# Moving the output projection, the layer norm and the convolution within a step, one PSUM bank for all attention sums, and other forms of a scan and a copy

## The chip, the cores and the metric

The kernel runs on one core of a Trainium2 chip. The metric is the time on the device for one execution, in microseconds (us); less is better. TensorE (PE), VectorE (DVE), ScalarE (ACT), GpSimd (POOL) and SyncE (SP) each work through a queue of their own in order; SP only issues DMAs here.

## The reference, cut to what matters

x has 16 images of 128 channels and 64 x 64 positions, so 4096 tokens each. Layer 0 is a group norm and a Mamba block, added to x. Layer 1 is an attention whose sums run over all earlier tokens, and then a routed feed-forward network (64 experts choose 8 tokens each).

```python
# layer 0: Mamba, 256 inner channels, 16 states
xz = gn(x) @ W_in; xs, z = split(xz)
xc = silu(causal_conv(xs, 4 taps) + conv_b)
dt, B, C = split(xc @ W_xproj)
delta = softplus(dt @ W_dt + b_dt)
h[t] = exp(delta[t]*A)*h[t-1] + (delta[t]*xc[t])*B[t]     # 16 states, 256 channels
y[t] = sum_n h[t]*C[t];  out = ((y + xc*D) * silu(z)) @ W_out;  x = x + out
# layer 1: attention with running sums, 8 heads
kv = silu(ln(t) @ W_kv);  s = q . k
m = cummax(s); e = exp(s - m); u = cumsum(e); w = cumsum(e*v)
t = t + mean_over_heads(w / u)
# then the routed feed-forward, added to t
```

## The kernel before

Three phases follow one another: layer 0 with the attention of layer 1 beside it (up to about 10090 us), the routing, and the experts with the final sums. The change touches the first phase alone.

**Steps.** A block is 512 tokens of one image; there are 16 x 8 = 128. The loop over `k` makes one step for each block, with the 16 states as its inner rounds `n`. In step k stand the scan of block k (`cur`), the end of layer 0 for block k - 1 (`prev`), the convolution and projections of block k + 1 (`nxt`), the attention of block m = k - 9 (`m`, whose second half ends in the next step as `mp_`), and the layer norm of block k - 8 (`mn`). So steps 0 to 8 have no attention; some ten steps at the end have no scan.

**A round.** In round n VectorE makes `bx` = delta*xc*B (`product`), then two scans of 512 tokens (`h`, one for each half of the channels). Between the two scans stands what `between(n)` emits: `score_less` at n = 4, `score_sum` at n = 6, `delta_x` at n = 15. POOL multiplies h with C into the tile `da`, which held the decay before, and copies the last column of h to `state`. At odd n `add_pair` has a DMA of POOL's queue add da of n - 1 to da of n; `add_y` lets TensorE turn and sum it into PSUM two rounds later. `decays` has ScalarE make the exponentials of up to two coming rounds; the variable LEAD limits how far ahead (8 rounds, in 13 da buffers). The queue of SP loads B and C of round n + 3 (`load_bc`, tile `bct`), 512 KB each.

**Everything else** is emitted by `beside(n)`, after `product(n)` and before the scans of the round. Each engine executes it in the order in which it is written, which was fixed by hand (`InOrder`), so the order of the calls is the order of each queue. What the prediction follows:

- `key`, `score`: keys of eight heads, then 32 x 2 small matmuls into `s_ps`; `score_max` (a running maximum, `mx`) and `score_less` on VectorE, `score_exp` on ScalarE, `score_sum` (a running sum, `sum`) on VectorE. Both running values are chained over chunks by `from_chunks` (two transposes, small scans on `z_max` or `z_sum`, and a copy of two columns).
- `score_log`, `rest`, `split`: the logarithm of the sums, and its split in three bf16 parts, which go back and forth between ScalarE and TensorE; `inverse` makes `e`; `turn_weights` turns the weights (`et_ps`); `store_parts` writes the parts to DRAM on ACT's queue, `spread_parts` reads them back on SP's queue with 16 small DMAs into `lh` and `rh`.
- `weights(c)` for each of four chunks: matmuls of lh and rh into two PSUM banks, exponentials by ScalarE into `wm`. `attend(c)`: 8 matmuls with wm, 16 small ones and one with `carry` for the sum over earlier chunks (`carry_ps`); `carry_on(c)` is its copy on ScalarE. `attend_before`, `add_x` and `finish` end a half of 256 tokens.
- `conv(nxt, a)`, eight matmul instructions for each half of the channels (`xs_ps`), `conv_silu` (tile `xc`), `xproj` (`dbl_ps`), `delta` (`dt_ps`), `gate_silu` (tile `z`).
- `turn_y` (`yb_ps`), `gate` (on VectorE, tile `z`), `out_proj` (`o_ps`, with the residual added by an identity matmul) and `put_back`, its copy on ScalarE.
- `ln_center`, `ln_square`, `ln_var`, `ln_scale` (tile `rstd`), `ln_apply` (tile `xn`, on VectorE): the keys of the next step read xn.

**PSUM.** Of eight banks three rotate as `bank(...)` for short results, two hold y, two hold bx, and one (`acc`) holds either the scores or the attention sums, one tile after the other.

Of the kernel before, what the change touches and what calls it, by code (L numbers as in the profile page):

```python
# [8 lines left out]
F32 = mybir.dt.float32  # L9
# [6 lines left out]
P = 128  # L16
# [23 lines left out]
def conv_attn_hybrid(ctx: ExitStack, tc: tile.TileContext, x, w_in, conv_w, conv_b, w_xproj, w_dt, b_dt,  # L40
# [40 lines left out]
    with ExitStack() as st:  # L81
        wp = st.enter_context(tc.tile_pool(name="wp", bufs=1))
        ps = st.enter_context(tc.tile_pool(name="ps", bufs=3, space=PSUM))
        acc = st.enter_context(tc.tile_pool(name="acc", bufs=1, space=PSUM))
# [49 lines left out]
        negc = wp.tile([P, 1], F32, name="negc")  # L134
        zs = {what: [wp.tile([P, 32], F32, name=f"z_{what}{a}") for a in range(2)] for what in ("max", "sum")}
# [70 lines left out]
        dap = st.enter_context(tc.tile_pool(name="dap", bufs=13))  # L206
# [92 lines left out]
        def gate_silu(k):  # L299
            w = blocks[k]  # L300
            z = w["z"] = m1.tile([P, NH2, L], F32, tag="z", name="z")
            for a in range(NH2):
                pt = bank("z_ps")
                PE.matmul(pt, wz[:, bass.ts(a, P)], w["xb"][:, KC - 1 :], start=True, stop=True)
                ACT.activation(z[:, a, :], pt, AF.Silu)
# [16 lines left out]
        def delta(k):  # L322
            w = blocks[k]
            d = w["delta"] = mp.tile([P, NH2, L], F32, tag="delta", name="delta")
            for a in range(NH2):
                pt = bank("dt_ps")
                PE.matmul(pt, wdt[:, bass.ts(a, P)], w["dbl"][:R, :], start=True, stop=True)
                softplus(d[:, a, :], pt, bdt[:, a : a + 1])
# [159 lines left out]
        def score(m, g):  # L488

            s = att[m]  # L490
            if g == 0:
                s["s"] = acc.tile([P, L], F32, tag="acc", name="s_ps")
            kt = [s.pop(("kt", 4 * g + j)) for j in range(4)]
            for c in range(CB):
                for j in range(4):
                    PE.matmul(s["s"][32 * j : 32 * j + 32, :P], q1[:, j, g, c, :], kt[j][:, bass.ts(c, P)],
                              start=(g == 0 and c == 0), stop=(g == 1 and c == CB - 1))

        def from_chunks(m, what, local, first, op0, op1, data):

            b, i = divmod(m, NBLK)
            last = stp.tile([P, 32], F32, tag=f"last_{what}", name=f"last_{what}")
            DVE.transpose(last, local[:, P - 32 :])
            z = zs[what][m % 2]
            if i == 0:
                DVE.memset(z[:, 0:10:5], first)
            else:
                DVE.tensor_copy(z[:, 0:10:5], gn[b][what][:, 4:14:5])  # L510
            gn[b][what] = z
            for g in range(2):
                DVE.tensor_tensor_scan(z[:, 5 * g + 1 : 5 * g + 5], bc(data[:, 0:1], [P, CB]),
                                       last[:, 5 * g : 5 * g + 4], z[:, 5 * g : 5 * g + 1], op0, op1)
            back = stp.tile([P, 32], F32, tag=f"back_{what}", name=f"back_{what}")
            DVE.transpose(back, z)
            return back[:, 31:32]

        def score_max(m):
            s = att[m]  # L520
            s["mx"] = a1.tile([P, P], F32, tag="mx", name="mx")
            DVE.tensor_tensor_scan(s["mx"], bc(negc, [P, P]), s["s"][:, :P], NEG, ALU.max, ALU.max)

        def score_less(m):
            s = att[m]
            mx = s.pop("mx")
            before = from_chunks(m, "max", mx, NEG, ALU.max, ALU.max, negc)
            x = s["x2"] = a1.tile([P, 2, P], F32, tag="x2", name="x2")
            DVE.scalar_tensor_tensor(x[:, 0, :], mx, before, s["s"][:, :P], ALU.max, ALU.subtract)
# [6 lines left out]
        def score_sum(m):  # L536
            s = att[m]
            s["sum"] = a1.tile([P, P], F32, tag="sum", name="sum")
            DVE.tensor_tensor_scan(s["sum"], bc(ones[:, 0:1], [P, P]), s["w"], 0.0, ALU.mult, ALU.add)
            s["before"] = from_chunks(m, "sum", s["sum"], 0.0, ALU.mult, ALU.add, ones)  # L540
# [25 lines left out]
        def rest(m, part):  # L566

            s = att[m]
            if part == 1:
                s["rest"] = bank("rest_ps")  # L570
                PE.matmul(s["rest"][:, : 2 * P], ident, s["x2"].rearrange("p w s -> p (w s)"), start=True, stop=False)
            PE.matmul(s["rest"][:, : 2 * P], minusb, s["parts"][:, part - 1].rearrange("p w s -> p (w s)"), start=False,
                      stop=True, skip_group_check=part > 1)
# [48 lines left out]
        def attend(m, c):  # L622
# [3 lines left out]
            if c % 2 == 0:  # L626
                s["o"] = acc.tile([P, L], F32, tag="acc", name="ao_ps")
# [44 lines left out]
        LEAD, LEAD_BC = 8, 3  # L672
# [37 lines left out]
        for k in range(NK + LAG + 1):  # L710
# [23 lines left out]
            def beside(n):  # L734
# [39 lines left out]
                if n == 4:  # L774
                    load_exp()
                    if m is not None:
                        score_max(m)
                    if mp_ is not None:
                        weights(mp_, 2)
                    if ends is not None:  # L780
                        gn_end(ends, 1)
                if n == 5:
                    if mp_ is not None:
                        attend(mp_, 2)
                        weights(mp_, 3)
                    if m is not None:
                        score_exp(m)
                    if prev is not None:
                        out_proj(prev)
                    decays(k, n, 2)  # L790
                    if mp_ is not None:
                        carry_on(mp_, 2)
                if n == 6:
                    if mp_ is not None:
                        attend(mp_, 3)
                        attend_before(mp_, 2)
                    if nxt is not None:
                        conv(nxt, 0)
                    decays(k, n, 2)
                    if prev is not None:  # L800
                        put_back(prev)
                    if mp_ is not None:
                        carry_on(mp_, 3)
                    if ends is not None:
                        gn_end(ends, 3)
                if n == 7:
                    if mp_ is not None:
                        attend_before(mp_, 3)
                        add_x(mp_, 1)
# [4 lines left out]
                    if m is not None:  # L814
                        split(m, 1)
                    if nxt is not None:
                        conv(nxt, 1)
                    if m is not None:
                        rest(m, 2)
                        inverse(m)  # L820
                    if mp_ is not None:
                        finish(mp_, 1)
                    if m is not None:
                        split(m, 2)
                        store_parts(m)
                    if nxt is not None:
                        conv_silu(nxt)
                    if ends is not None:
                        gn_end(ends, 4)
                if n == 8:  # L830
                    if m is not None:
                        turn_weights(m)
                        value(m, 0, 0)
# [3 lines left out]
                    if m is not None:  # L837
                        value(m, 0, 1)
                if n == 9:
                    if mn is not None:  # L840
                        ln_center(mn)
                        ln_square(mn)
# [6 lines left out]
                if n == 10:  # L849
                    if mn is not None:  # L850
                        ln_var(mn)
                    if nxt is not None:
                        delta(nxt)
                    load_exp()
                    if mn is not None:
                        ln_scale(mn)
                if n == 12:
                    if m is not None:
                        weights(m, 0)
                if n == 13:  # L860
                    if m is not None:
                        attend(m, 0)
                        attend_before(m, 0)
                        weights(m, 1)
                    decays(k, n, 2)
                    if m is not None:
                        carry_on(m, 0)
                if n == 14:
                    if mn is not None:
                        ln_apply(mn)  # L870
# [3 lines left out]
                    if m is not None:  # L874
                        carry_on(m, 1)
                if n == 15:
                    if stat is not None:
                        gn_stats(*stat)

            for n in range(N):  # L880
# [5 lines left out]
                if n in (4, 11, 12, 15):  # L886
                    decays(k, n, 2)
# [13 lines left out]
                if 8 <= n <= 11 and i == 0 and prev is not None:  # L901
                    store_residual(b - 1, n - 8)
                if 14 <= n <= 15 and i == 0 and cur is not None:
                    load_residual(b, n - 14)
                if n < 2 and i == 1 and cur is not None:
                    load_residual(b, n + 2)
                if n == 7 and mn is not None:
# [302 lines left out]
```

## Time and profile before

| what | us |
|---|---|
| median of 3 runs | 10935.1 |
| lowest and highest | 10931.48 and 10961.1 |
| profiled execution | 10931.22 |
| its span | 10929.5 |

The span runs from the first to the last instruction. The profile gives for each group of instructions its count, its mean duration and what ended the idle time ahead of it; the timeline gives single instructions as start, duration, engine, line, operation, output and inputs. Every operation of the first phase bears the line of the helper `InOrder` (L31), so rows are told apart by tiles. Adjacent instructions of one kind are merged to a row with their count; a 32-bit matmul counts as two. A TensorE row's end is modelled, and rows overlap a little; distances from start to start are safer.

### The profile page before, as it was taken

The page shows a single profiled execution, that of the slowest core. Times are in us where ns is not written, and L with a number is a line of the kernel's source. Part 1 is how long each engine was busy: PE and PEld are TensorE (multiplying, and loading weights), DVE is VectorE, ACT ScalarE, POOL GpSimd, SP SyncE. Part 2 cuts the span into 40 slices and gives each one's busy share as a digit, 9 for nine tenths or more (in the row PEclk, how much of TensorE's full clock was granted, in tenths as well). Part 3 has the DMA queues.
Part 4 walks back from the last instruction along what each step waited for, and adds up shares of the span by engine and source line. Part 5 has one row for each costly group of instructions (what it writes and reads, how often), then busy time and mean ns, then how long its engine had stood idle before and what let it go on. Part 6 is the DMA issues. An engine that isn't in the chain of part 4 may idle for free.

```text
span 10929.5 us, 157776 instructions
## 1 busy us (share of the span) xinstructions
PE 9405.6 (86%) x55389; PEld 5549.3 (51%) x55389; DVE 9012.1 (82%) x9987; ACT 7284.5 (67%) x12924; POOL 7530.3 (69%) x4771
## 2 busy tenths in 40 slices
PE   4579998899988989998899999989899899888875
PEld 2345555555555555555555555555555555544752
DVE  8998888888888888888889888888888888820753
ACT  5567776777777777777777777777777777754640
POOL 7887777778777777777777777777777777820000
PEclk7789998999999999899998998999999899999886
DMA  7777767777677777776777777677777777721348
GB/s 191 199 205 182 198 178 199 181 193 184 179 199 181 195 179 195 185 195 181 187 190 184 194 181 200 176 199 180 193 187 176 198 178 192 184 65 34 109 154 343
DMA packets 944361, 1995.67 MB, mean 183 GB/s; under 512 B 103040, under 2 KB 188688, under 8 KB 936400
## 3 DMA queue, kind: packets, MB, share of 16 engines
q1 hardware_dynamic: 732912, 1414.88, 43.6%
q0 software_dynamic: 129024, 469.82, 22.0%
q10 hardware_dynamic: 81632, 100.88, 2.7%
q8 instruction: 439, 7.19, 0.3%
q14 instruction: 354, 2.90, 0.1%
HBM read 1363.98 MB, written 151.52 MB: 139 GB/s over the span
## 4 chain that ended last, share of the span: by engine, by line
PE 61%; ACT 18%; DVE 7%; DMA 7%; issue 5%; SPq 1%; ACTq 1%; POOL 1%; DVEq 0%; POOLq 0%
PE ao_ps L31 10%; PE k_ps L31 8%; PE v_ps L31 7%; PE xs_ps L31 7%; PE y_ps L31 6%; ACT da L31 5%; PE carry_ps L31 4%; PE o_ps L31 4%; DVE h L31 3%; PE s_ps L31 3%; ACT L219 3%; ACT wm L31 2%; PE dt_ps L31 2%; DVE bx L31 2%; PE dbl_ps L31 2%
## 5 line engine op out<-in xcount | busy, mean ns | idle before, releaser
L31 POOL TENSOR_TENSOR da<-h,bct 128x1024 f32<-128x1024 f32 x2048 | 6475.5, 3162 | 1943.1 <-DVE h L31 1521.5
L31 DVE TENSOR_TENSOR_SCAN h<-da,state,bx 128x512 f32<-128x512 f32 x3584 | 4414.6, 1265 | 169.5 <-DVE bx L31 3.4
L31 DVE TENSOR_TENSOR bx<-du,bct 128x1024 f32<-128x1024 f32 x2048 | 2598.3, 1269 | 470.3 <-DMA bct<-bcs 404.1
L31 ACT ACTIVATE da<-delta,a_neg 128x512 f32<-128x512 f32 x4096 | 2629.8, 716 | 89.5 <-DMA da<-da 61.4
L31 PE MATMUL y_ps<-ident,da 128*128 128x128 f32 x9216 | 1428.1, 309 | 279.2 <-DMA da<-da 278.9
L31 PEld LDWEIGHTS y_ps<-ident,da 128*128 128x128 f32 x9216 | 1210.5, 160 | 719.6 <-issue 401.8
L31 PE MATMUL ao_ps<-wm,v 128*128 128x128 f32 x8192 | 1266.4, 318 | 281.5 <-ACT wm L31 276.4
L31 PEld LDWEIGHTS ao_ps<-wm,v 128*128 128x128 f32 x8192 | 1182.1, 226 | 559.8 <-ACT wm L31 401.8
L31 PE MATMUL v_ps<-wv,xn 128*128 128x512 f32 x2048 | 1035.8, 629 | 257.0 <-ACT xc L31 240.9
L31 ACT ACTIVATE v<-v_ps 128x512 f32<-128x512 f32 x1024 | 606.3, 597 | 778.7 <-PE v_ps L31 669.1
L31 ACT ACTIVATE wm<-w_ps 128x512 f32<-128x512 f32 x1024 | 552.1, 590 | 608.7 <-PE w_ps L31 607.3
L31 PE MATMUL k_ps<-xn,wk 128*128 128x512 f32 x2048 | 944.4, 595 | 1.7 <-ACT kt L31 1.7
L31 PE MATMUL xs_ps<-xb,wc 128*128 128x512 f32 x2048 | 925.3, 595 | 1.8 <-issue 1.8
L31 POOL DMA_DIRECT2D da<-da x896 | 787.7, 879 | 163.9 <-POOL state L31 95.1
L31 PEld LDWEIGHTS v_ps<-wv,xn 128*128 128x128 f32 x2048 | 341.9, 192 | 787.5 <-issue 316.1
L31 ACT ACTIVATE kt<-k_ps 128x512 f32<-128x512 f32 x1024 | 587.3, 600 | 190.0 <-PE k_ps L31 166.2
L31 DVE TENSOR_TENSOR_SCAN h<-da,bx 128x512 f32<-128x512 f32 x512 | 599.8, 1206 | 25.5 <-ACT da L31 0.5
L31 PEld LDWEIGHTS xs_ps<-xb,wc 128*128 128x128 f32 x2048 | 372.0, 191 | 397.1 <-issue 382.5
L31 ACT ACT_TABLE_LOAD x395 | 506.8, 1283 | 51.6 <-ACT parts L31 45.9
L31 PEld LDWEIGHTS k_ps<-xn,wk 128*128 128x128 f32 x2048 | 371.6, 191 | 321.0 <-issue 254.7
L31 POOL COPY state<-h 128x2 f32<-128x2 f32 x1792 | 509.0, 284 | 0.0
L31 DVE TENSOR_TENSOR z<-yb_ps,z 128x512 f32<-128x512 f32 x256 | 164.8, 685 | 339.7 <-PE yb_ps L31 339.3
(196 smaller groups left out, 10931.1 us busy)
## 6 DMA issues: line engine op xcount, KB each, us to landing
bct<-bcs SPq DMA_DIRECT2D x2048, 512.0 KB
da<-da POOLq DMA_DIRECT2D x896, 512.0 KB, 8.1
xs<-t_d SPq DMA_DIRECT2D x240, 256.0 KB
xs<-in_x_dram SPq DMA_DIRECT2D x128, 256.0 KB
xt<-in_x_dram SPq DMA_DIRECT2D x64, 512.0 KB
t_d<-xt SPq DMA_DIRECT2D x64, 512.0 KB
t_d<-xs ACTq DMA_DIRECT2D x256, 128.0 KB
t<-t_d SPq DMA_DIRECT2D x128, 256.0 KB
```

What stands on the lines that cost most here:

```text
L31: return lambda *args, **kw: self.tc.keep_in_program_order(f(*args, **kw))
L219: tc.keep_in_program_order(nc.scalar.preload_act_table_set(EXP_LN))
```

## The change

All calls of the diff stay what they compute; what differs is where they stand, which buffers they use, and the form of two VectorE operations.

- One PSUM tile `shared` takes the place of `acc` and lives through the phase: its first 256 columns hold the attention sums and `rest`, the third 128 the scores, the last 128 zeros, written once.
- The running sum adds w and those zeros; it no longer reads a broadcast column of ones from SBUF. The copy in `from_chunks` becomes a reduction over an axis of length one.
- In `beside`: the convolution's halves go from n = 6 and 7 to n = 4 and 6, `out_proj` and `put_back` from n = 5 and 6 to n = 10, the layer norm from n = 9, 10 and 14 to n = 13, 14 and 15, `weights(m, 0)` from n = 12 to 11, `attend(m, 0)` and `attend(m, 1)` from n = 13 and 14 to n = 12 and 13. The last half of the attention of the block before ends at n = 6 and not at n = 7. At n = 7 `conv_silu` stands ahead of `turn_weights` and the second split.
- `delta` issues its matmuls for both halves, then both softplus.
- z has two buffers, da has 12, LEAD is 7.
- Loads and stores of the residual and one load of x stand in other rounds.

```diff
-        acc = st.enter_context(tc.tile_pool(name="acc", bufs=1, space=PSUM))
+        bank1 = st.enter_context(tc.tile_pool(name="bank1", bufs=1, space=PSUM))
...
+        shared = bank1.tile([P, L], F32, name="shared")
+        nc.vector.memset(shared, 0.0)
...
-        dap = st.enter_context(tc.tile_pool(name="dap", bufs=13))
+        dap = st.enter_context(tc.tile_pool(name="dap", bufs=12))
...
-            z = w["z"] = m1.tile([P, NH2, L], F32, tag="z", name="z")
+            z = w["z"] = m1.tile([P, NH2, L], F32, tag="z", name="z", bufs=2)
...
+            pt = [bank("dt_ps") for _ in range(NH2)]
             for a in range(NH2):
-                pt = bank("dt_ps")
-                PE.matmul(pt, wdt[:, bass.ts(a, P)], w["dbl"][:R, :], start=True, stop=True)
-                softplus(d[:, a, :], pt, bdt[:, a : a + 1])
+                PE.matmul(pt[a], wdt[:, bass.ts(a, P)], w["dbl"][:R, :], start=True, stop=True)
+            for a in range(NH2):
+                softplus(w["delta"][:, a, :], pt[a], bdt[:, a : a + 1])
...
-                s["s"] = acc.tile([P, L], F32, tag="acc", name="s_ps")
+                s["s"] = shared[:, 2 * P : 3 * P]
...
-                DVE.tensor_copy(z[:, 0:10:5], gn[b][what][:, 4:14:5])
+                DVE.tensor_reduce(z[:, 0:10:5], gn[b][what][:, 4:14:5].unsqueeze(2), mybir.AxisListType.X, ALU.max)
...
-            DVE.tensor_tensor_scan(s["sum"], bc(ones[:, 0:1], [P, P]), s["w"], 0.0, ALU.mult, ALU.add)
+            DVE.tensor_tensor_scan(s["sum"], s["w"], shared[:, 3 * P :], 0.0, ALU.add, ALU.add)
...
-                s["rest"] = bank("rest_ps")
+                s["rest"] = shared
...
-                s["o"] = acc.tile([P, L], F32, tag="acc", name="ao_ps")
+                s["o"] = shared
...
-        LEAD, LEAD_BC = 8, 3
+        LEAD, LEAD_BC = 7, 3
```

The order in `beside` after the change, from n = 4, the conditions left out:

```python
n == 4:  load_exp(); score_max(m); weights(mp_, 2); conv(nxt, 0); decays; gn_end(ends, 1)
n == 5:  attend(mp_, 2); score_exp(m); carry_on(mp_, 2); attend_before(mp_, 2); weights(mp_, 3); decays
n == 6:  conv(nxt, 1); attend(mp_, 3); attend_before(mp_, 3); add_x(mp_, 1); decays
         carry_on(mp_, 3); finish(mp_, 1); gn_end(ends, 3)
n == 7:  score_log(m); rest(m, 1); decays; split(m, 1); inverse(m); conv_silu(nxt)
         turn_weights(m); rest(m, 2); split(m, 2); store_parts(m); gn_end(ends, 4)
n == 8:  xproj(nxt); store_bc(nxt); value(m, 0, 0), value(m, 0, 1)
n == 9:  gate_silu(cur); load_block(k + 2, ACT); value(m, 1, 0), value(m, 1, 1)
n == 10: delta(nxt); out_proj(prev); load_exp(); put_back(prev)
n == 11: weights(m, 0); decays
n == 12: attend(m, 0); attend_before(m, 0); carry_on(m, 0); weights(m, 1); decays
n == 13: ln_center(mn); ln_square(mn); attend(m, 1); decays; carry_on(m, 1)
n == 14: ln_var(mn); ln_scale(mn); decays
n == 15: ln_apply(mn); gn_stats(*stat); decays
```

And the transfers:

```diff
-                if 8 <= n <= 11 and i == 0 and prev is not None:
-                    store_residual(b - 1, n - 8)
-                if 14 <= n <= 15 and i == 0 and cur is not None:
-                    load_residual(b, n - 14)
-                if n < 2 and i == 1 and cur is not None:
-                    load_residual(b, n + 2)
-                if n == 7 and mn is not None:
+                if 12 <= n and i == 0 and prev is not None:
+                    store_residual(b - 1, n - 12)
+                if 2 <= n <= 5 and i == 1 and cur is not None:
+                    load_residual(b, n - 2)
+                if n == 10 and mn is not None:
                     load_x(mn, True)
```

## The prediction

> **What bounds the kernel now.** The page comes first:
>
> ```profile
> PE 9405.6 (86%) x55389; PEld 5549.3 (51%) x55389; DVE 9012.1 (82%) x9987; ACT 7284.5 (67%) x12924; POOL 7530.3 (69%) x4771
> ...
> PEclk7789998999999999899998998999999899999886
> ```
>
> TensorE and VectorE are both nearly full, and TensorE runs at about 0.91 of its clock in the main loop (windows view). So shares don't decide; I look for the cycle that repeats. In 1000 to 9000 us TensorE's wait for the convolution's SiLU occurs 105 times, so a step of the main loop with attention takes 8000/105.5 = 75.8 us. The first eight steps, without attention, go from 45.46 to 562.87 us: 64.7 us each, VectorE without a pause. What stops VectorE later is read from its waits between 700 and 9500 us:
>
> ```profile
> DVE bx L31 <- DMA bct<-bcs: 397.2, 128, 11.1
> DVE z L31 <- PE yb_ps L31: 319.4, 105, 5.3
> ```
>
> That is 716 us over some 116 steps, 6.2 us a step; the rest, 69.6 us, is VectorE's own work. Then one plain step in the timeline, VectorE:
>
> ```profile
> 4433.75 0.35 DVE L31 SCALAR_TENSOR_TENSOR x<-mx,back_max,s_ps 128x128 f32<-128x128 f32 x1
> ...
> 4441.73 1.17 DVE L31 TENSOR_TENSOR_SCAN sum<-ones,w 128x128 f32<-128x128 f32 x1
> ...
> 4476.42 1.23 DVE L31 TENSOR_TENSOR bx<-du,bct 128x1024 f32<-128x1024 f32 x1 [4.54 <-DMA bct<-bcs]
> 4477.56 0.68 DVE L31 TENSOR_TENSOR xn<-cen_ps,rstd 128x512 f32<-128x512 f32 x1
> ...
> 4501.33 1.29 DVE L31 TENSOR_TENSOR z<-yb_ps,z 128x512 f32<-128x512 f32 x2 [2.16 <-PE yb_ps L31]
> ...
> 4506.16 0.41 DVE L31 TENSOR_TENSOR_SCAN mx<-negc,s_ps 128x128 f32<-128x128 f32 x1
> ...
> 4507.77 0.70 DVE L31 COPY z_max<-z_max 128x2 f32<-128x2 f32 x1
> ...
> 4509.15 0.35 DVE L31 SCALAR_TENSOR_TENSOR x<-mx,back_max,s_ps 128x128 f32<-128x128 f32 x1
> ```
>
> From score_less (end 4434.10) to the next (4509.50) are 75.4 us. Two pauses: 4.54 us at n=14, where the bct load sits on SP behind spread_parts, and 2.16 us at n=3, where the gate waits for TensorE. The same step on TensorE:
>
> ```profile
> 4438.92 1.98 PE L31 MATMUL o_ps<-z,wo 128*128 128x512 f32 x4 [0.74 <-ACT wm L31]
> ...
> 4450.97 3.60 PE L31 MATMUL xs_ps<-xb,wc 128*128 128x512 f32 x8
> 4454.40 0.27 PE L31 MATMUL rest_ps<-parts,minusb 128*128 128x256 bf16 x1
> 4455.14 0.33 PE L31 MATMUL et_ps<-ident,w 128*128 128x128 f32 x1 [0.46 <-ACT parts L31]
> 4457.51 1.24 PE L31 MATMUL v_ps<-wv,xn 128*128 128x512 f32 x2 [2.04 <-ACT xc L31]
> 4458.68 3.44 PE L31 MATMUL dbl_ps<-xc,wx 128*40 128x512 f32 x4
> ...
> 4478.90 3.65 PE L31 MATMUL ao_ps<-wm,v 128*128 128x128 f32 x16 [0.54 <-ACT wm L31]
> ```
>
> The reader is to see that o_ps (3.52 us with its residual) and the second convolution (3.44) stand exactly where ScalarE has work to finish, and that after a gap matmuls take up to double: dbl_ps 3.44 us against 1.91 in the step at 4078.98, ao_ps 3.65 against 1.97 at 4442.44.
>
> [...]the 128x128 scan takes 1.17 us from SBUF (sum) and 0.41 from PSUM (mx); the two-column copy 0.70 us in the max chain, 0.13 in the sum chain.[...]
>
> **The change, part by part.** VectorE first. The sum scan loses 1.17 - 0.41 = 0.76 us, the copy about 0.55 (0.70 to the 0.13 of the same copy[...]; between 0.1 and 0.2 for the new form). The zeroing of the bank happens once (0.27 us by lh's memset). VectorE's own work falls from 69.6 to 68.3.
>
> The order matters more. After the change I follow one chain around a step, at full clock, with durations and start-to-start distances from the timeline; A is the end of the second add_x, W the start of weights(m, 0), X the moment xn can be made.
>
> 1. score_less to A. All attention sums share one bank, so attend(2) starts after score_less: attend 3.02, attend_before 0.22, weights(3) with the wait for its first exponential 1.47 (the distance 4437.45 to 4438.92; the convolution needs that buffer as o_ps did), conv(1) 3.44, attend(3) 2.79, attend_before 0.22, add_x 0.59, handover 0.15: 11.9.
> 2. A to the x-projection. The zeros of the sum scan lie in the bank that TensorE writes, [...] it now runs 7.6 us after score_less (4441.73). New wait of 12.0 - 7.6 = 4.4 us; behind it stand the rest of n=6 and everything later on VectorE, and POOL, which waits for each h. Then 0.1 + 0.41, the sum chain 0.90, log and cast 0.8, decays 2.46, split 0.27, inverse 1.17, table load 1.30, first SiLU 0.64: 8.1. TensorE has only add_y, rest and et here: some 5 us idle, since conv(1) no longer stands in it.
> 3. x-projection to W: x-projection 1.84, four values 3.62, z 1.72, four dt matmuls 2.0 (0.78 of wait gone by issuing them together), o_ps 3.52, add_y twice 1.75: 14.45. SP's spread has to land too: store_parts comes at A+9.4, the last issue was 13.0 us after the store (4455.11 to 4468.09), landing about 15 (estimate): A+24.4 against A+22.55. Hidden if the clock drops.
> 4. W to X: exponentials at 0.76 to 1.7, decays to 4.2, carry_on(0) after attend(0) at 4.65, weights(1), exponentials 5.4 to 6.4, decays to 8.85, square, decays to 11.9, carry, Ln, Exp: 13.5. Layer norm now ends this chain; before, it was finished beside n=11.
> 5. X to the next score_less: xn 0.60, statistics 0.60, h and du 4.0, three rounds of 3.85, round 3 with the gate 4.9, round 4 to score_less 3.9 (0.55 already off): 25.6.
>
> Sum 11.9 + 8.1 + 14.45 + 13.5 + 25.6 = 73.6 us. To that comes the clock. Before, 9% of 75.8 us, 6.8, is lost to it. After: the idle 5 us at n=7 and 8 slow x-projection and values, 1.5 to 3 us (the shorter gap of before costs dbl_ps 1.5); the dt matmuls [...]the slow stretch starts beside them today, so o_ps may be slowed, 0 to 3; attend(2), after a wait for the pair of n=1, 0 to 1.7. I take 2.1 + 1.2 + 0.7 = 4.0, bounds 1.5 and 7.7. **Step: 77.6 us**, bounds 75.1 and 81.3.
>
> VectorE alone would reach xn at 46.4 after score_less (12.0, the rest of n=6 2.5, eight rounds 30.7, bx 1.2); X is at 51.9 with the clock, so it waits 5.5 us there. The gate's 2.16 and bct's 4.54 disappear (TensorE reaches the keys early; VectorE comes later), but X is late in their place.
>
> What I cost at nothing: LEAD 7 and 12 da buffers (da 15 is made at n=11, some 4 us before use; if that cover goes, VectorE waits at n=15, where it waits anyway). z's second buffer, needed because the new z is made before the old is used. Residual loads and stores and load_x (0.42 to 0.47 us each on SP) move off n=8 to 11, where a step with stores shows a 9.30 us bct wait; that step's gain is covered by X. The ACT queue's store_parts is counted in 3; POOL's issues stay. The first nine steps stay at VectorE's 64.7. In the nine or ten last steps layer norm is no longer beside values: about 2 us each, 20.
>
> 119 steps x (77.6 - 75.8) = 214, plus 20: 10931.2 + 234 = 11165 for the profiled execution (span 10929.5), which lies 4 us under the median of the runs; I say 11160.
>
> **Rivals.**
> - *Layer norm comes in time, VectorE bounds* (faster). If X is at 46.4 or before, a step is 46.4 + 25.6 = 72.0: 119 x -3.8 + 20 = -430, 10500. It decides from X under 50.2, where a step is 75.8. For it: TensorE's 7.4 us of waits a step and much of its clock loss can go, since o_ps follows dt. Against: items 2 and 4 are ScalarE's order and contain three pairs of decays ahead of Ln. Part of it, X between 47 and 50, is likelier: 10550 to 10920.
> - [...](columns tracked): the sum is early, log follows add_x at once, 0.65 us less in item 2: 76.9 us, 11080. The sign stays.
> - *The clock at its bound*: attend(2) and o_ps slowed as well, 80 us: about 11450.
> - [...]the new forms cost what the old did, 0.76 us in item 2 and 0.55 in item 5: 78.9, 11320. The two equal pairs of rows above speak against it.
>
> **Numbers.** My forecast 0.45, columns tracked 0.15, clock at its bound 0.10[...]: with their spread, slower by over 0.3% (33 us, about what a measurement of this kernel can tell) 0.75. X in time, wholly or in part, 0.20. Within 0.3% 0.05. The range goes from 10800, half of the faster case, to 11420.
>
> **What would show it.** Right: VectorE's waits name rstd before xn (some 5 us a step) and TensorE before sum (some 4), none for yb_ps; v_ps or dbl_ps wait for xc some 3 us after a gap; sum near 0.4 us, the z_max form under 0.2. Wrong: xn without a wait and a step under 75 us; a granted clock above 0.97 would go with it.

## The result, and the profile after

| | before | after |
|---|---|---|
| median, us | 10943.76 | 11685.1 |
| lowest and highest, us | 10931.48 to 10961.1 | 11648.47 to 11725.02 |
| profiled execution, its span, us | 10931.22, 10929.5 | 11693.64, 11691.9 |
| a step (mean distance of the `du` products, steps 20 to 110 of the trace), us | 75.8 | 82.3 |

The change makes the kernel slower: ratio 1.0677, 95% interval 1.0637 to 1.0717. The prediction was 11160, with a range up to 11420; the sign was right and the size was not. The span grew by 762 us: over all 118 steps with attention and a scan the mean distance is 81.9 against 75.7, which gives some 730, and the stretch after the last `du` took 34 us more.

The page, shares and clock:

```profile
PE 9296.3 (80%) x55389; PEld 5400.8 (46%) x55389; DVE 8878.5 (76%) x9988; ACT 7307.2 (62%) x12924; POOL 7351.2 (63%) x4771
...
PEclk7789999999999999999999999999999999989886
```

The work did not grow: PE, DVE and POOL are busy for 109, 134 and 179 us less than before, and ScalarE for only 23 us more. The time went into waits. VectorE's and TensorE's waits between 1000 and 9000 us (total, how often, longest); the 97 occurrences mean 97 steps, so dividing by 97 gives the wait in a step:

```profile
DVE sum L31 <- ACT xs L31: 600.6, 97, 9.8
DVE xn L31 <- ACT rstd L31: 461.9, 97, 9.2
DVE bx L31 <- DMA bct<-bcs: 322.1, 115, 5.7
...
PE dbl_ps L31 <- ACT xc L31: 278.6, 97, 2.9
PE w_ps L31 <- DMA rh<-pd: 268.2, 110, 5.5
```

VectorE waits 6.2 us before sum, 4.8 before xn and 3.3 for bct: 14.3 us a step, so its own work is about 68.0 us, where 68.3 were predicted. The last row is the one that the prediction did not have: TensorE waits for rh, which the spread loads, 2.8 us a step.

VectorE in one step, in the timeline (start, duration, in brackets the idle time ahead and what ended it), with the ScalarE row that the sum waits for:

```profile
4413.01 0.35 DVE L31 SCALAR_TENSOR_TENSOR x<-mx,back_max,shared 128x128 f32<-128x128 f32 x1
...
4426.47 0.42 DVE L31 TENSOR_TENSOR_SCAN sum<-w,shared 128x128 f32<-128x128 f32 x1 [5.45 <-ACT xs L31]
...
4457.59 1.70 DVE L31 TENSOR_TENSOR bx<-du,bct 128x1024 f32<-128x1024 f32 x1 [1.83 <-DMA bct<-bcs]
4466.72 0.69 DVE L31 TENSOR_TENSOR xn<-cen_ps,rstd 128x512 f32<-128x512 f32 x1 [3.58 <-ACT rstd L31]
...
4490.03 0.11 DVE L31 TENSOR_REDUCE z_max<-z_max 128x2 f32<-128x2 f32 x1
...
4491.21 0.35 DVE L31 SCALAR_TENSOR_TENSOR x<-mx,back_max,shared 128x128 f32<-128x128 f32 x1
```

```profile
4426.05 0.38 ACT L31 ACTIVATE xs<-shared 128x256 f32<-128x256 f32 x1 [0.39 <-PE shared L31]
```

The sum takes 0.42 us instead of 1.17, the reduction 0.11 instead of the copy's 0.70, as predicted. But the sum starts 13.1 us after score_less, at the end of finish's read of the bank, where it stood 7.6 us after it before. The gate no longer waits for yb_ps.

TensorE in the same step:

```profile
4425.42 0.60 PE L31 MATMUL shared<-xs,ident_hd 128*128 128x256 f32 x2
...
4434.62 3.63 PE L31 MATMUL dbl_ps<-xc,wx 128*40 128x512 f32 x4 [2.90 <-ACT xc L31]
...
4451.35 0.39 PE L31 MATMUL w_ps<-rh,lh 64*128 64x512 bf16 x1
4453.44 0.37 PE L31 MATMUL w_ps<-rh,lh 64*128 64x512 bf16 x1 [1.70 <-DMA rh<-pd]
```

The reader is to see the last add_x (first row), the doubled x-projection after the gap, and weights(m, 0) cut in two by the wait for rh. From 4434.62 to 4438.25, during this x-projection, TensorE's granted clock was 0.50; in the kernel before the one at 4078.98, with 1.91 us, had 1.00. And SP, which issues the spread:

```profile
4436.29 4.18 SPq L31 DMA_DIRECT2D bct<-bcs  x2
4440.52 1.14 SPq L31 DMA_DIRECT2D xs<-t_d  x1
4441.77 0.30 SPq L31 DMA_DIRECT2D lh<-pd  x1
...
4442.79 0.41 SPq L31 DMA_DIRECT2D rh<-pd  x1
4446.77 0.23 SPq L31 DMA_DIRECT2D lh<-pd  x1
```

Four issues go out 0.35 us apart, then nothing for 4 us. Call this hole the hold. SP's own waits name what ends it:

```profile
SPq L31 <- POOL state L31: 4910.4, 1014, 15.5
...
SPq L31 <- DMA bct<-bcs: 400.8, 125, 6.1
```

The first row is that of the bct loads, which wait until POOL has freed a buffer. The second row has nothing to do with data: the spread doesn't read bct. The trace also gives, for every DMA, the semaphore (a counter on which instructions can wait) that counts its landing. All 5585 DMAs that SP and ScalarE issue in this trace share eight of them, numbered 101 to 108; in the median the eighth DMA after one takes the same semaphore again. In all 5577 cases in which one was taken again, the issue came after the DMA that had it before had landed, at least 0.016 us later. Here the fifth DMA of the spread (4446.77) takes semaphore 102, which the second of the two bct loads, issued at 4440.11, had; that load landed at 4446.75. In 52 of 60 steps (40 to 100) the longest pause lies ahead of the fifth issue and ends 0.02 us after that load has landed; in the other 8 the landing of another of these DMAs (the bcs store or the load of xb) ends it. So the hold is a wait for a semaphore, and no property of the DMA queues needs to be assumed for it.

### The profile page after: what moved, and what is told of

Same layout as the page of the kernel before. It is cut to its first block, busy times and chain, and to the rows that moved or that the text cites. A ratio compares the mean times of both kernels' runs of the same rounds, so it can differ in the third digit from the quotient of the medians.

```text
span 11691.9 us, 158415 instructions
## 1 busy us (share of the span) xinstructions
PE 9296.3 (80%) x55389; PEld 5400.8 (46%) x55389; DVE 8878.5 (76%) x9988; ACT 7307.2 (62%) x12924; POOL 7351.2 (63%) x4771
## 4 chain that ended last, share of the span: by engine, by line
PE 32%; DVE 22%; DMA 17%; ACT 12%; issue 9%; POOL 6%; SPq 2%; DVEq 0%; ACTq 0%; POOLq 0%
DVE h L31 10%; PE shared L31 9%; DVE bx L31 7%; PE xs_ps L31 7%; POOL da L31 6%; DMA bct<-bcs 6%; ACT da L31 5%; PE v_ps L31 4%; DMA da<-da 4%; PE carry_ps L31 3%; PE w_ps L31 3%; DMA lh<-pd 3%; DMA rh<-pd 2%; ACT wm L31 2%; SPq L31 1%
## 5 line engine op out<-in xcount | busy, mean ns | idle before, releaser
L31 POOL TENSOR_TENSOR da<-h,bct 128x1024 f32<-128x1024 f32 x2048 | 6394.7, 3123 | 2841.4 <-DVE h L31 1433.1
L31 PEld LDWEIGHTS y_ps<-ident,da 128*128 128x128 f32 x9216 | 1089.7, 146 | 791.7 <-issue 439.1
L31 PE MATMUL y_ps<-ident,da 128*128 128x128 f32 x9216 | 1241.5, 282 | 263.5 <-DMA da<-da 263.3
L31 PE MATMUL v_ps<-wv,xn 128*128 128x512 f32 x2048 | 1130.3, 680 | 223.8 <-DVE z L31 218.2
L31 PE MATMUL shared<-wm,v 128*128 128x128 f32 x8192 | 1148.4, 300 | 116.6 <-ACT wm L31 114.6
L31 PEld LDWEIGHTS shared<-wm,v 128*128 128x128 f32 x8192 | 1102.0, 212 | 289.7 <-ACT wm L31 201.9
L31 PEld LDWEIGHTS v_ps<-wv,xn 128*128 128x128 f32 x2048 | 413.5, 219 | 930.5 <-issue 490.2
L31 PE MATMUL dbl_ps<-xc,wx 128*40 128x512 f32 x512 | 457.8, 1049 | 360.2 <-ACT xc L31 360.2
L31 DVE TENSOR_TENSOR_SCAN sum<-w,shared 128x128 f32<-128x128 f32 x128 | 53.8, 420 | 853.7 <-ACT xs L31 853.7
L31 DVE TENSOR_TENSOR xn<-cen_ps,rstd 128x512 f32<-128x512 f32 x128 | 88.5, 691 | 748.0 <-ACT rstd L31 748.0
```

The lines of the kernel that those rows point to most:

```text
L31: return lambda *args, **kw: self.tc.keep_in_program_order(f(*args, **kw))
```

## The experiments

Times are medians with the ratio to the kernel before and its 95% interval. Two numbers describe the hold, medians over steps 40 to 100: the longest distance between two neighbouring issues of the spread, and the last issue counted from the issue of store_parts. Other positions within a step are means over steps 20 to 110, since means add up to the step: a median would hide that the sum starts near 13.1 us after score_less in some steps and near 14.8 in others.

**1. The sum alone.** The kernel after, with the old form of the scan:

```diff
-DVE.tensor_tensor_scan(s["sum"], s["w"], shared[:, 3 * P :], 0.0, ALU.add, ALU.add)
+DVE.tensor_tensor_scan(s["sum"], bc(ones[:, 0:1], [P, P]), s["w"], 0.0, ALU.mult, ALU.add)
```

> The changed kernel with the old form of the running sum (ones and w from SBUF), so that score_sum no longer reads the shared bank and waits neither for add_x nor for finish. Theory 'chain' (a step of 82.5 us is the cycle score_less, attend, add_x, log, convolution's SiLU, x-projection, spread of the parts, attend, Ln, xn, score_less): the sum's wait of 6.2 us a step is slack that the wait at xn hides; only the log comes earlier, behind finish instead of behind the sum, about 1.0 us a step: 11565, and the wait of xn for rstd grows from 4.8 to about 9 us a step. Rival 'sum': the sum's wait on the shared bank is the loss itself; 5 us or more a step come back: about 11000 to 11100, the wait of xn unchanged.

Measured: 11065.41, ratio 1.0118 (1.0092 to 1.0145), 76.5 us a step. My expectation failed; the rival's number came. Yet xn still waits:

```profile
DVE xn L31 <- ACT rstd L31: 425.1, 105, 8.0
```

so layer norm still ends the step, and still xn came 5.7 us earlier, of which the earlier x-projection is 1.1. On TensorE the wait for rh is nearly gone:

```profile
PE w_ps L31 <- DMA rh<-pd: 9.5, 6, 2.8
```

and on SP the spread goes out in one go, here 6.9 us after the end of the last two bct issues:

```profile
4492.39 4.17 SPq L31 DMA_DIRECT2D bct<-bcs  x2
...
4503.45 0.26 SPq L31 DMA_DIRECT2D lh<-pd  x1
4503.76 0.29 SPq L31 DMA_DIRECT2D rh<-pd  x1
```

SP's wait for the landing of bct loads falls from 400.8 us to 48.6. The reason is the time at which the last bct load ahead of the spread goes out: 22.4 us after score_less in the kernel before, 22.3 in this run, 27.6 in the kernel after. In all 90 steps of each of the three, what lets it go is POOL, which frees its buffer.

**2. The layer norm alone**, all of it back to n = 11, ahead of weights(m, 0):

```diff
 if n == 11:
+    ln_center(mn); ln_square(mn); ln_var(mn); ln_scale(mn)
     weights(m, 0)
```

> The changed kernel with the whole layer norm up to rstd at n=11, ahead of weights(m, 0); xn stays at n=15. Theory 'chain': rstd is ready at about 43 us after score_less and not at 56.8, the wait at xn goes, and VectorE's own order with the sum's wait and the bct wait is the next bound: about 76.7 us a step, 10950 to 11100. Rival 'sum': nothing is gained but what xn waited beyond the sum's wait, and a new wait replaces it: 11500 or more. Rival 'TensorE' (the loss is TensorE's clock and gaps): 11500 or more as well, with TensorE's waits unchanged.

Measured: 11292.62, ratio 1.0314 (1.029 to 1.0338), 78.9 us a step: between the two. The wait before xn vanishes from VectorE's waits, but the wait before sum grows:

```profile
DVE sum L31 <- ACT xs L31: 696.9, 101, 8.5
```

Layer norm was the chain's last link. Without it the waits left to VectorE are those for the sum (6.9 us a step) and for bct (3.4); that score_less, attend(2), add_x and sum make the next loop is read from them and not tested.

**3. The store earlier.**

```diff
 split(m, 1)
+rest(m, 2); split(m, 2); store_parts(m)
 inverse(m); conv_silu(nxt); turn_weights(m)
-rest(m, 2); split(m, 2); store_parts(m)
```

> The changed kernel with the second split and store_parts straight after the first split, ahead of inverse and the convolution's SiLU. Theory 'chain': the parts are stored 3.5 us earlier, so lh and rh land 3.5 us earlier, while the x-projection starts 1.2 us later; weights(m, 0) then waits for TensorE's own order and its exponentials come 1.0 us earlier: about 11575. If the spread isn't on the chain the 1.2 us later are all that is seen: 11830. Rival 'sum': no difference, 11690.

Measured: 11493.11, ratio 1.0503 (1.0482 to 1.0524), 80.4 us a step. The direction was right, and half of the gain came as expected: counted from the sum, the x-projection comes 1.3 us later and the first exponential of weights(m, 0) 1.0 us earlier. But the way there was another: the store goes out 3.5 us earlier, the last issue of the spread only 1.5, since a bct load still stands 1.2 us ahead of it and the hold is still 2.9 us. The other half was not expected. TensorE no longer waits for rh, the sixteen wm matmuls of attend(0) take 2.1 us instead of 3.0, and from that exponential to xn are 12.6 us instead of 13.6. That part I put down to TensorE's clock: in the kernel after, these matmuls take 2.1 us at a granted clock of 1.00 and 2.9 to 3.8 at 0.50 to 0.70.

**4. The reduction alone**, in the kernel before:

```diff
-DVE.tensor_copy(z[:, 0:10:5], gn[b][what][:, 4:14:5])
+DVE.tensor_reduce(z[:, 0:10:5], gn[b][what][:, 4:14:5].unsqueeze(2), mybir.AxisListType.X, ALU.max)
```

> The kernel before with only the copy of two columns replaced by the reduction. VectorE saves 0.55 us a step ahead of score_less. Theory: in the kernel before VectorE waits for TensorE at the gate and for bct, so most of it turns into these waits; between 0 and 0.3 us a step, 10900 to 10945. If VectorE's own time bounded it, 0.55 us x 119 = 65 us would come: 10875.

Measured: 10933.32, ratio 0.9992 (0.9983 to 1.0), as expected. The reduction takes 0.115 us where the copy took 0.709 (medians). Of these 0.59 us the step shows 0.1 (75.7 us against 75.8); 0.4 are found again as waits between 1000 and 9000 us, bct with 435.9 us instead of 362.2 and yb_ps with 261.0 instead of 289.7.

**5. The lateness without the bank.** The sum from SBUF as in 1, but VectorE first copies one column of what finish(mp, 1) wrote:

```diff
+DVE.tensor_copy(tick, xs_of_finish[:, 0:1])
 score_sum(m)
```

> The kernel after with the sum in its old SBUF form (which took 0.4 us a step less by itself than its place would say), but ahead of it VectorE copies one column of what finish(mp, 1) has written, so that the sum stands as late as in the kernel after[...]. Theory (it is the lateness of VectorE at n=6 that costs, by way of POOL and the bct loads; the bank only causes it): the step comes back to 82.5 and some 0.6 to 0.8 us for the slower sum: 11,680 to 11,790. Rival 'reading the bank costs in some other way' (TensorE's or ScalarE's accesses slowed by it): near the kernel with the sum from SBUF, 11,065 to 11,200.

Measured: 11674.82, ratio 1.0665 (1.063 to 1.0701), 82.1 us a step; the longest distance within the spread is 4.5 us again, as in the kernel after (4.5; in 1 it is 1.1). The time is 5 us below the range that I gave, since the sum from SBUF takes 0.42 us at this place and not 1.19 as in run 1. One copied column brings back all that 1 had won:

```profile
DVE tick L31 <- ACT xs L31: 600.7, 97, 9.6
```

The last bct load again goes out 27.7 us after score_less. So no access to the bank as such costs the time; it is that VectorE is late at n = 6.

**6. No new spread.** Weights read the parts of the step before, spread at n = 6:

```diff
-if n == 10 and m is not None: spread_parts(m)
+if n == 6 and mp_ is not None: spread_parts(mp_)
```

> The kernel after, with one thing left out: weights use the parts that the step before stored, so spread_parts is issued at n=6 and TensorE never waits for rh (the weights are those of the step before; everything else is computed as in the kernel after). Theory (of the 5.9 us a step that the late sum costs, some 2.7 come by the spread's landing and some 1.6 by TensorE's clock after that wait): step 78 to 79 us, about 11,230 to 11,300; the bx wait for bct at n=14 nearly gone. Rival 'the spread hides beside o_ps' (as the prediction had it): within 0.5 us of the kernel after, 11,640 to 11,690. Rival 'all of it is the spread': 76.6, 11,065.

Measured: 11085.72, ratio 1.0125 (1.011 to 1.014), 77.2 us a step. I expected 78 to 79; it is nearly the "all of it". The waits for rh and bct are gone; those before sum (656.5 us) and xn (346.3 us) stay.

**7. The spread ahead of one bct load.** In the kernel after, round 10:

```diff
+if n == 10 and m is not None: spread_parts(m)
 load_bc(*order[later])
...
-if n == 10 and m is not None: spread_parts(m)
```

> The kernel after with one thing moved: in round 10 SP issues the 16 DMAs of spread_parts ahead of the bct load for round 13, not behind it. Theory (in the kernel after, the late sum makes POOL free the bct buffer late, so that a 512 KB bct load goes out right ahead of the spread and holds its DMAs back for some 4 us): the hold goes, rh lands some 4 us earlier, TensorE no longer waits for rh before w_ps, and the step comes near that of the kernel whose weights need no new spread (77.2 us): 78 to 79 us, 11,200 to 11,350. The bct loads come later by 6 us, but VectorE waits for rstd behind them anyway. Rival 'the spread is slow because of its own 16 small DMAs': the hold stays, 11,600 to 11,690. Rival 'bct is then late': the wait before bx grows by over 4 us a step and the time stays over 11,550.

Measured: 11371.77, ratio 1.0396 (1.0372 to 1.0419), 79.2 us a step: near the theory's step, some 20 us beyond its range. Last issue 13.5 us after the store instead of 16.5, and no wait for rh is left among TensorE's. The hold itself shrinks only to 3.2 us. Another DMA is the one waited for now: in 58 of 60 steps the seventh issue of the spread waits until ScalarE's store to bcs, which had its semaphore, has landed. And part of the gain is given back: bct comes late, and so does the summed da:

```profile
SPq L31 <- DMA bcs<-dbl: 281.9, 100, 4.0
...
DVE bx L31 <- DMA bct<-bcs: 399.6, 161, 5.2
...
PE y_ps L31 <- DMA da<-da: 239.8, 144, 3.8
```

**8. Half the bytes.** In the kernel after, each bct load brings 256 KB instead of 512, with no change in order or number:

```diff
-SP.dma_start(t, w["bcs"][n : n + N + 1 : N, :].partition_broadcast(P))
+SP.dma_start(t[:, 0:1, :], w["bcs"][n : n + 1, :].partition_broadcast(P))
```

> The kernel after with bct loads of half the bytes: only B is loaded (256 KB), and POOL multiplies h with B in place of C, so the sums of layer 0 are others; every instruction count stays. Theory (a bct load under way when the spread's DMAs are issued holds their issue until its bytes are moved): the hold of 4.4 us in the middle of the spread's 16 issues falls to 2 us or less, TensorE's wait for rh before w_ps goes from 2.4 us a step to below 0.5, VectorE's wait for bct goes, and the step is 77.5 to 79.5 us, 11,100 to 11,380. Rival 'the count of DMAs or packets holds it, whatever their size': the hold stays, and the time lies within 1% of the kernel after, over 11,570.

Measured: 11146.85, ratio 1.0183 (1.0166 to 1.0201), 77.3 us a step. The same place on SP:

```profile
4454.12 0.30 SPq L31 DMA_DIRECT2D lh<-pd  x1
...
4455.10 0.28 SPq L31 DMA_DIRECT2D rh<-pd  x1
4456.72 0.23 SPq L31 DMA_DIRECT2D lh<-pd  x1
```

Again four issues, then a hole, but of 1.6 us (median 1.7) instead of 4; last issue 13.4 us after the store. TensorE's wait for rh falls from 268 us to 1.3, and VectorE's wait for bct is gone. The last bct load ahead of the spread lands 3.6 us after its issue, where it took 7.0 in the kernel after (medians of 60 steps): with half the bytes the hold is 1.7 us instead of 4.5. That it is mostly the fifth issue in the kernel after (52 of 60 steps) comes from which DMA has which of the eight semaphores. More semaphores, or another order of the DMAs between the load and the spread, were not tried.

**9. Both undone.** The sum of 1 and the layer norm of 2 together:

> Both parts that moved the time alone are undone together: the sum reads SBUF again, and the whole layer norm stands at n=11. Theory (one chain with two independent joints: the sum's wait delays everything from the log on, and layer norm is the chain's last link): alone they gave 5.9 and 3.8 us a step; together X lies some 5.9 + 6 us earlier than in the kernel after, VectorE no longer waits for it, and what is left is VectorE's own work (about 69 us with the slower sum) plus the wait for bct (some 3.5 us): 72.5 to 74 us a step, 10,600 to 10,800 us, faster than before. Rival 'one and the same slack' (the two gains are the same idle time taken twice): about 76 us a step, 11,000 to 11,060. Rival 'TensorE bounds': the wait before the sum or the gate comes back and a step stays over 75 us.

Measured: 10876.96, ratio 0.9935 (0.992 to 0.995), 75.2 us a step: faster than before, but less than I expected. What came is the rival 'TensorE bounds', with a step over 75 us and the gate's wait back: VectorE waits for bct 456.7 us and for yb_ps 174.4. TensorE waits for ScalarE at xc, parts and kt for 736 us in these 8000, so the loop over these two engines is the likely bound; run 12 tests it.

**10. The same with the store earlier** (the edit of 3):

> As the one before, and at n=7 the second split and store_parts stand ahead of inverse and conv_silu, so that the spread is issued some 2 us earlier. Theory (16 spread DMAs and the 512 KB loads of bct get in each other's way on SP): the wait for bct at n=14 goes down from about 3.5 to about 1 us, as it did when the store alone was moved; 71 to 72 us a step, 10,450 to 10,600. Rival 'bct waits for something else than the spread': no difference to the run without it, within 0.3%.

Measured: 11112.19, ratio 1.0155 (1.0138 to 1.0172), 77.3 us a step: slower, against both expectations. Moving the store ahead of the SiLU makes the x-projection 1.4 us later, on the loop that now bounds. And ScalarE's own issue of the bcs store comes into the stretch in which the spread is issued. In the step shown (one of 50 such waits, 179.7 us in all) it needs the semaphore of the spread's first rh, waits until that has landed, and holds ScalarE's computing behind it:

```profile
4472.44 1.09 ACT L31 ACTIVATE v<-v_ps 128x512 f32<-128x512 f32 x2 [3.92 <-DMA rh<-pd]
```

**11. Two loads ahead of the spread**, in the kernel of 9: round 10 issues the bct loads for rounds 14 and 15 ahead of the spread, and rounds 11 and 12 issue none.

> The kernel with the sum from SBUF and the layer norm at n=11 (10,877 us, 75.1 us a step, VectorE waits 3.3 us a step for bct at n=13), with the bct loads for rounds 14 and 15 issued ahead of the spread, not behind it. Theory (TensorE and ScalarE bound that kernel by their own loop: keys, scores, score_less, attend): the bct wait falls below 1.5 us a step, but the gate's wait for yb_ps grows in its place: 74 to 75 us, 10,740 to 10,870. Rival 'VectorE with its bct wait bounds it': 72 us, about 10,500. Rival 'a load right ahead holds the spread', as in the kernel after: w_ps waits for rh, over 10,950.

Measured: 11414.86, ratio 1.0434 (1.0415 to 1.0454), 79.8 us a step: the third rival's time, by another way. VectorE waits for bct no more, and the last issue of the spread moves from 11.4 to 17.0 us after the store. But w_ps waits for rh only 34.9 us, 16 times. It is ScalarE that is held, when it issues the load of xb: in 87 of 100 steps that DMA has to wait until a bct load which had its semaphore has landed:

```profile
ACT v L31 <- DMA bct<-bcs: 358.2, 87, 6.3
```

That is 4.1 us each time. TensorE then waits for ScalarE before dt_ps (230.2 us), and the first exponential of weights(m, 0) comes 4.6 us later after the x-projection than in run 9.

**12. inverse later**, in the kernel of 9: from n = 7, ahead of conv_silu, to n = 10, after the table load and ahead of put_back.

> The same kernel (sum from SBUF, layer norm at n=11) with the four exponentials of inverse (1.27 us on ScalarE) moved from n=7, where they stand ahead of the convolution's SiLU, to n=10, where ScalarE waits for o_ps. Theory (TensorE waits for xc at n=8, on the loop that bounds the step): the x-projection starts 1.3 us earlier and TensorE's stretch at half clock gets shorter too; step 73.4 to 74.2, 10,660 to 10,770. Rival 'VectorE's bct wait bounds it': no difference, within 0.3% of 10,877.

Measured: 10768.05, ratio 0.9842 (0.9825 to 0.9859), 74.2 us a step: as expected, at the slow end of the range, and the fastest kernel of this study. That TensorE's slow stretch gets shorter hardly shows: the granted clock of the whole run is 0.929, against 0.928 in run 9. The x-projection starts 1.3 us earlier; its wait for xc shrinks from 306.3 us to:

```profile
PE dbl_ps L31 <- ACT xc L31: 184.5, 108, 1.7
```

**13. The edits of 11 and 12 together.**

> Both moves in one: bct loads for rounds 14 and 15 ahead of the spread, and inverse at n=10. Theory (two joints that take turns: TensorE's loop and the bct load): 72.5 to 73.5 us a step, 10,550 to 10,680, under each alone. Rival 'the held spread': as the run with the loads first alone, or slower than it.

Measured: 11452.55, ratio 1.0467 (1.0448 to 1.0485): the rival. As long as the loads stand ahead, moving inverse gains nothing (38 us more than run 11).

## Why the prediction was right in sign and wrong in size

*VectorE's own work and the forms* were right: 68.0 us against 68.3, sum 0.42, reduction 0.11. The 0.1 to 0.2 us for the reduction were an estimate, since the kernel before has none in this place. That the old forms are slowed by POOL beside them is now better shown: in the kernel before, the same scan from SBUF takes 1.18 us in the 119 blocks in which a multiplication of POOL overlaps it and 0.42 in the last nine, where none does; the copy of two columns takes 0.71 us in the max chain with such an overlap and 0.13 in the sum chain, which never has one. The last nine blocks have no scan of layer 0 beside them at all, but run 5 shows the same in the main loop: there the old form stands as late as the sum of the kernel after, no multiplication overlaps it in 127 of 128 blocks, and it takes 0.42 us. In the kernel after none overlaps the sum in 127 of 128 blocks either. So the sum's new form gains nothing by itself where it now stands.

*Item 1 and the new wait of the sum* were right in kind. That the sum would wait for A was an assumption of mine that the trace of the kernel before doesn't show; in the kernel after it waits for ScalarE's read behind A in all 97 steps between 1000 and 9000 us. The sum starts 14.0 us after score_less; the prediction's sum gives 12.7 (11.9 for A, 0.1, and the clock's 0.7), so 1.3 are missing. Two things were left out: add_y of round 1 stands ahead of attend(2), in some steps after the rest of the first convolution, and attend(2) begins 1.6 us after score_less; and the sum waits for finish's read of the bank too, 0.45 us after A instead of 0.1. The clock's 0.7 did not come: the sixteen wm matmuls of attend(2) take 2.0 us. The sum's wait is 6.2 us a step instead of 4.4.

*Item 2* was right: 8.15 us from sum to x-projection against 8.0, with a wait for xc of 2.9 where some 3 was said.

*Item 3 failed*, in this sentence: the spread lands at A+24.4, "Hidden if the clock drops." The clock did drop, in the x-projection (3.6 us instead of 1.84, at a granted clock of 0.50, means of steps 20 to 110), and TensorE stood ready for the second matmul of weights(m, 0) at A+26.4. But its rh came only at A+28.9. The store went out at A+9.6, as predicted (A+9.4); the issues took longer. I had carried over the 13.0 us from store to last issue from the kernel before, where the last bct load left 5.6 us ahead of the spread (median). After the change it leaves 1.4 us ahead of it. The change makes VectorE late at n = 6; POOL follows and frees the bct buffer late, so this load goes out 27.6 us after score_less and not 22.4. It lands 7.0 us after its issue, and the spread's fifth DMA, which needs its semaphore, waits for that: 16.5 us from store to last issue. From x-projection to the first exponential of weights(m, 0) a step took 21.2 us, and the prediction's sum has 18.5 (14.45, 3.3 of the clock, and 0.76 to that exponential): 2.7 us too few. So the new wait, costed as one on the chain alone, also moved a load in front of the spread. Runs 5, 6, 7 and 8 show this link by link: lateness without the bank, no wait for the spread, another order, fewer bytes.

*Item 4 and the clock* followed. From the first exponential of weights(m, 0) to xn are 13.6 us instead of 12.7 (13.5 less the 0.76). TensorE has just waited for rh, and attend(0) runs slowly: its sixteen wm matmuls take 3.0 us at a granted clock of 0.72 (means), and 2.1 us in runs 1, 3, 6 and 8, where the same stretch takes 12.5 to 12.7 us. Within the kernel after it goes with the wait: in steps 20 to 110 they take 2.1 us at a granted clock of 1.00 in all 26 steps with less than 1.5 us of waits for rh, and 2.9 to 3.8 us at 0.50 to 0.70 (mean 0.54) in all 50 with more than 2. My bounds for the clock did not name this place, since I had no wait there. Where they did name one, behind the dt matmuls, nothing was lost: the four matmuls of o_ps with z take 2.0 us, as before. That o_ps might be slowed there was an estimate, from the slow stretch beside the dt matmuls of the kernel before (granted clock 0.50 from 4472.04 to 4482.28, in the step that the prediction shows).

*Item 5* was right: 25.3 against 25.6.

Together: 1.3 + 0.15 + 2.7 + 0.9 - 0.3 = 4.7 us, from 77.6 to 82.3. When the hold is taken away, the step is near the prediction's sum: 77.2 us in run 6, 77.3 in run 8. That it agrees so well is in part luck. In run 8 item 1 is 1.25 us longer than predicted and item 3 about 1.05 shorter (17.45 us), and the two cancel. Against run 8 the hold costs 3.75 us in item 3 and 1.2 in item 4, the whole 5.0 us between the two kernels. So the chain was the right one; the term for the spread was mis-sized and took the clock with it. What the prediction costs at nothing (LEAD, z's second buffer, the other places of the residual transfers) was not run by itself; these moves are all in runs 6 and 8 too.

*What was to show it*: rstd before xn with 4.8 us (5 predicted), ScalarE behind TensorE before sum, no wait for yb_ps, xc 2.9: all there. Wrong is "bct's 4.54 disappear": 3.3 us a step are left, since SP issues the next bct loads behind the spread and so late as well; in runs 6 and 8 this wait is gone. The tail took 34 us more, not 20.

*The rivals*: that columns are tracked is refuted, as the wait before sum shows. The clock at its bound did not come, since attend(2) and o_ps were not slowed (2.0 us each). The last rival (0.05 of the weights), that POOL has no part in the slow scan and copy, is refuted above. Layer norm in time alone (run 2) did not make VectorE the bound at 72 us, since the sum's wait grew to 6.9 us a step; it needs the sum's wait undone as well, and even then TensorE's and ScalarE's loop ends at 75.2.

My expectation of run 1 failed for the same reason as the prediction: I priced the sum's wait by what it delays on ScalarE and did not follow it to POOL and SP.

## What to carry to other kernels

A wait that a change adds must be followed through every engine behind it to the DMA queues: what it makes late there may now collide with a transfer that used to be alone. A landing time read from a trace is valid only with the same transfers ahead of it; give it a range when the change shifts them. When an issue stands still, look which semaphore it needs and which DMA had it before: a DMA can wait for one with which it shares no data. When one of two in-order loops is shortened, work out what the other allows (75.2 us in run 9) before counting the whole gain, and look for work in front of its waits, as inverse in run 12.

## What the runs showed of the hardware

- VectorE's 128 x 128 scan with both inputs in SBUF was slowed by a multiplication of POOL beside it: 1.18 us with one in the kernel before, 0.42 without one in run 5. The scan `mx`, with one input in PSUM, takes 0.41 us in the 119 blocks with POOL beside it. The two-column copy takes 0.71 us with and 0.13 without one, the reduction in its place 0.115 in both cases.
- In the kernel after, the bct load of 512 KB ahead of the spread landed 7.0 us after its issue, in run 8 one of 256 KB after 3.6 us (medians of 60 steps).
- After TensorE waited for more than 2 us for rh, sixteen 128 x 128 fp32 matmuls took 2.9 to 3.8 us at a granted clock of 0.50 to 0.70 (50 steps of the kernel after), and 2.1 us at 1.00 in the 26 steps with less than 1.5 us of such waits.
- VectorE's sum and ScalarE's read of other columns of the same PSUM bank, both reads, ran one after the other: finish's read ended at 4426.43, the sum began at 4426.47. In the trace the sum waits for a semaphore of ScalarE; no run leaves that wait out with the zeros in this bank. Against a start 0.1 us after A it cost about 0.35 us a step. The zeros in another bank were not tried.
